# A group norm's sums taken through memory instead of the matrix engine, PSUM emptied ahead of other work, and some products issued in halves

## The chip, the cores and the metric

The kernel runs on one core of a Trainium2 chip. The metric is the device time of one execution in microseconds (us). Engines are named as in the profile: PE (TensorE, matmuls), PEld (its weight loads), DVE (VectorE), ACT (ScalarE), POOL (GpSimd) and SP (SyncE, which issues most DMAs). All data is float32. A float32 matmul appears in the profile as two passes (two MATMUL records) and two weight loads.

## The reference

Sixteen elements of 256 channels by 1024 positions go through two layers. Cut to what matters:

```python
# layer 0: attention of 4 heads of 64 over 1024 positions, biases, residual
q, k, v = split(xs @ w_proj + b_proj)
x = softmax(q k^T * 64**-0.5) v @ w_out + b_out + xs
# layer 1
x = x + attention(group_norm(x, gn1_w, gn1_b), 8 heads of 32, proj, phys_bias)
h = gelu(mlp_w1 @ group_norm(x, gn2_w, gn2_b) + mlp_b1)     # 1024 hidden channels
x = x + mlp_w2 @ h + mlp_b2
# group_norm: 32 groups of 8 channels, mean and variance over 8 x 1024 values,
#             (x - mu) / sqrt(var + 1e-5) * w + b
```

The norm that the change touches is the first group_norm, between the two attentions.

## The kernel before

**Tiling.** Channels lie on partitions: 256 channels are two chunks (cc or ch) of 128 partitions, positions two halves (t) of TB = 512. The loop over the elements b holds, for each, attention a (layer 0), a stretch of full-array products, and attention b (layer 1); the MLP of element b - 1 is computed inside the turn of element b. Elements 1 to 14 are treated alike (`seven`); the first and the last have their own paths. In the attentions PE works in small tiles of the array (64x64, 32x64, 128x32); in the stretch between them it works with the whole array (128*128).

**The stretch between the attentions.** On PE it holds, for an inner element: the first half of the MLP of the element before (`begin`, `middle`, `finish`, four units i each, `products_of`, L1209), the output projection of attention a (`out_proj`, L381), the two small products of the norm, and then the query and key projections of the next element's layer 0 ("a") and of this element's layer 1 ("b").

**Projections by seven products.** `qk_by_seven` computes the 2x2 blocks of queries and keys with seven block products instead of eight. A piece is named layer, product, chunk: a20 is product 2 of chunk 0 for layer a. Each piece is one matmul of 128x512 (`mm`, L1108) and what follows: products 1 and 7 start a PSUM area, 6, 2, 4, 5, 3 accumulate into one. ACT copies two of the results aside (L1137, L1141) and one within PSUM (L1132); keys leave by ACT (L1116, L1118), queries by DVE (L1122 for b, L1124 for a). The inputs' sums t1 to t4 are made by DVE (`input_sums`, L1088 to L1091). The order of the pieces is written out in the main loop as a string of names.

**The norm.** `out_proj` adds the residual (L821) and takes statistics per channel (L825). `group_norm` joins them (`bn_aggr`, L894), and a product with a matrix of group averages, `gavg`, gives each channel the mean of its group: `gm_g` for the means, then on DVE the deviation, squared and added (L906 to L908), then `gv_g` for the variances (L915). `pow` on POOL (L916) gives the reciprocal root, three small DVE instructions scale and shift (L918 to L922), and four DVE instructions of 128x512 write the normed element (L928).

**The MLP's hidden units.** `finish(i)` adds two PSUM results on DVE (L1265, L1266), applies gelu to them on ACT (L1224), and forms two differences on DVE (L1285).

**What sets the order.** `Later` holds callbacks for a number of steps (`wait` in `group_norm`), so instructions are emitted between the pieces. A scheduler of the framework then orders each engine's instructions by its own estimates; `keep_in_program_order` and `issue_after` bind it. Each engine executes its own list in that order, and waits for the others by semaphores. SP's DMAs are one such list: between the last transfers of attention a (`row_a`, `d_a`, L422 and L427) and the load of the MLP's second weights (L315) it issues nothing.

**PSUM.** Three double areas (`wide`) and two single banks (`bank`) are handed round; a matmul that takes an area waits until the instructions that read it have run.

Of the kernel before, what the change touches and what calls it, by code (L numbers as in the profile page):

```python
# [8 lines left out]
F32 = mybir.dt.float32  # L9
I32 = mybir.dt.int32  # L10
AF = mybir.ActivationFunctionType
ALU = mybir.AluOpType
AX = mybir.AxisListType

P = 128
# [268 lines left out]
def first_pass(ctx, tc, x, out, k):  # L284
# [3 lines left out]
    HC = k["m1b"].shape[1]  # L288
    later = Later()
# [579 lines left out]
    def group_norm(key, src, stats, gw, gb, tag, out_tile, wait, then=None):  # L869
# [21 lines left out]
        def means():  # L891
            mv = small.tile([P, CC, 2], F32, tag="mv", name=f"mv_{key}")
            for cc in range(CC):
                nc.vector.bn_aggr(mv[:, cc, :], stats[:, cc].rearrange("p t k -> p (t k)"))  # L894
            mean_c = small.tile([P, CC], F32, tag="mean_c", name=f"mean_c_{key}")
# [15 lines left out]

        def apply():
            rstd = small.tile([P, CC], F32, tag="rstd", name=f"rstd_{key}")
            for sl, ps in averages(f"gv_{key}", st["tv"], False):
                nc.vector.tensor_scalar(rstd[sl], ps, EPS, None, ALU.add)  # L915
            nc.gpsimd.tensor_tensor(rstd, rstd, k["mhalf"], ALU.pow)  # L916
# [3 lines left out]
            nc.vector.tensor_mul(ma, st["mean"], a)  # L920
# [3 lines left out]
            out_tile.append(y)  # L924

# [10 lines left out]
            for t in range(NT):  # L936
                for cc in range(CC):
                    part(cc, t)
# [7 lines left out]
    def qkv(key, D, src, weights, b_qk, qT, kT, v_dst):  # L946
        def qk(ch, which, t):
            ps = single(f"qk_{key}_{ch}_{which}_{t}")
            for cc in range(CC):
                product(  # L950
                    ps,
                    weights(cc, which)[:, ch * P : (ch + 1) * P],
                    src[:, cc, t * TB : (t + 1) * TB],
                    start=(cc == 0),
                    stop=(cc == CC - 1),
                )
# [34 lines left out]
    def qkv_0(b, xb):  # L991
# [5 lines left out]
        def v():  # L997
# [7 lines left out]
            k["bqk"], q, kk, v,  # L1005
        )

    def qkv_1(b, xn):
# [6 lines left out]
            None, q, kk, lambda: v,  # L1015
# [67 lines left out]
    def input_sums(key, y):  # L1083
# [7 lines left out]
        nc.vector.tensor_sub(t4, b21, t2)  # L1091
        return dict(t1=t1, t2=t2, t3=t3, t4=t4, b11=b11, b21=b21, b22=b22)

    made_k = []

    def qk_by_seven(key, block, s, x, q, kk, bias=None):
# [10 lines left out]
        def mm(to, w, right, first):  # L1107
            ins = nc.tensor.matmul(  # L1108
                to, w, x[right], start=first, stop=True, skip_group_check=not first
            )  # L1110
            if ps:
                tc.keep_in_program_order(ins)
# [7 lines left out]
        def leave_q(to, what, more, ch):  # L1120
            if bias is None:
                nc.vector.tensor_add(to, more, what)  # L1122
            else:
                nc.vector.scalar_tensor_tensor(  # L1124
                    to, what, bias[:, 0, ch : ch + 1], more, ALU.add, ALU.add
                )
# [12 lines left out]
        def p6(ch):  # L1139
            mm(ps[ch][1], s[:, ch, 1], "t2", False)  # L1140
            nc.scalar.copy(aside_for()[:, 2 * ch + 1], ps[ch][1])  # L1141
# [5 lines left out]
        def p4(ch):  # L1147
            mm(ys[ch], block(0, ch, 1), "t4", False)
# [732 lines left out]
```

## Time and profile before

| | |
|---|---|
| median of 3 runs | 3586.73 us (3586.65 to 3588.13) |
| the profiled execution's own time | 3587.91 us |
| its span | 3586.1 us |
| PE busy | 3573.3 us, 35713 passes |
| DVE busy | 2785.1 us |
| ACT busy | 2288.7 us |
| POOL busy | 220.1 us |
| granted PE clock | 1.0 |
| DMA | 198.07 MB, mean 55 GB/s |

The page has the busy time of each engine, the span in 40 slices, the DMA queues, the chain of work that ended last, and groups of instructions with the idle time ahead of them and what ended it. In a timeline, each line has the start (us from the span's start), the duration, the engine, the source line, and the tiles written and read; in brackets the idle time ahead and its releaser. An end of a matmul is modelled; the starts are used here.

### The profile page before, as it was taken

What the parts mean: (1) busy time and instruction counts of PE and PEld (TensorE: products, weight loads), DVE (VectorE), ACT (ScalarE), POOL (GpSimd) and SP (SyncE); (2) the same over time, 40 slices, a digit from 0 to 9 for tenths busy, and PEclk for the clock granted to TensorE, in tenths of its full rate; (3) what the DMA queues carried; (4) which work ended last, traced back from release to release, by engine and by line L of the source; (5) the groups of instructions that cost most, each with busy time, mean ns of one, the idle gap of its engine ahead of it and who ended that gap; (6) DMA issues with size and microseconds to landing.
All of it is one profiled execution on the core that took longest, in us unless ns stands there. A gap on an engine that the chain in (4) does not pass through costs nothing.

```text
span 3586.1 us, 82054 instructions
## 1 busy us (share of the span) xinstructions
PE 3573.3 (100%) x35713; PEld 1479.0 (41%) x35713; DVE 2785.1 (78%) x3188; ACT 2288.7 (64%) x3186; POOL 220.1 (6%) x319
## 2 busy tenths in 40 slices
PE   9999999999999999999999999999999999999999
PEld 4334344343444434444344443444434444344434
DVE  5786877868788687886868878688786877869787
ACT  5665757567575675856658566585765757657573
POOL 4000000001000010000000000000000100000000
PEclk9999999999999999999999999999999999999999
DMA  4011312213122131221312213121121211213100
GB/s 134 8 58 33 82 51 40 72 39 82 45 44 68 39 82 45 52 65 35 82 45 52 66 34 81 45 55 63 39 77 45 55 63 43 72 45 64 52 28 28
DMA packets 81606, 198.07 MB, mean 55 GB/s; under 512 B 38006, under 2 KB 38774, under 8 KB 75094
## 3 DMA queue, kind: packets, MB, share of 16 engines
q1 hardware_dynamic: 71860, 164.13, 15.0%
q0 software_dynamic: 7632, 28.21, 5.1%
q8 instruction: 282, 4.62, 0.5%
q14 instruction: 86, 0.70, 0.1%
q10 hardware_dynamic: 1746, 0.40, 0.1%
HBM read 125.59 MB, written 22.27 MB: 41 GB/s over the span
## 4 chain that ended last, share of the span: by engine, by line
PE 93%; DVE 4%; DMA 1%; issue 1%; SPq 0%; ACT 0%; DVEq 0%
PE s_b L642 13%; PE s_a L458 13%; PE acc_a L481 12%; PE acc_b L696 12%; PE m L1209 9%; PE m L381 9%; PE qk_a L1108 3%; PE qk_b L1108 3%; PE v_b L381 3%; PE j L381 3%; PE v_a L381 3%; PE o L381 3%; PE qk7y_b L1108 1%; PE qk7y_a L1108 1%; DVE es_b L670 1%
## 5 line engine op out<-in xcount | busy, mean ns | idle before, releaser
L655 ACT ACTIVATE e_b<-s_b 128x1024 f32<-128x1024 f32 (+1 forms) x1280 | 982.1, 864 | 135.3 <-PE s_b L642 135.3
L670 DVE TENSOR_TENSOR es_b<-es_b,e_b 128x2048 f32<-128x2048 f32 (+1 forms) x460 | 881.5, 1934 | 105.0 <-ACT e_b L655 88.6
L468 ACT ACTIVATE e_a<-s_a 128x1024 f32<-128x1024 f32 x512 | 521.2, 1025 | 359.1 <-PE s_a L458 356.3
L458 PE MATMUL s_a<-q,k 64*64 64x512 f32 x4096 | 544.3, 593 | 0.0
L481 PE MATMUL acc_a<-e_a,v 64*64 64x512 f32 x4096 | 540.1, 589 | 0.0
L642 PE MATMUL s_b<-q,k 32*64 32x512 f32 x8192 | 523.4, 600 | 2.7 <-ACT v L978 1.3
L495 DVE TENSOR_TENSOR es_a<-es_a,e_a 128x1024 f32<-128x1024 f32 x384 | 471.8, 1229 | 63.7 <-ACT e_a L468 42.9
L696 PE MATMUL acc_b<-e_b,v 128*32 128x512 f32 x4096 | 492.1, 598 | 0.0
L381 PE MATMUL m<-g,w 128*32 128x256 f32 (+1 forms) x6432 | 401.8, 384 | 0.0
L381 PEld LDWEIGHTS m<-g,w 128*32 128x32 f32 x6432 | 218.7, 111 | 205.0 <-issue 54.8
L481 PEld LDWEIGHTS acc_a<-e_a,v 64*64 64x64 f32 x4096 | 187.9, 133 | 251.5 <-issue 222.9
L642 PEld LDWEIGHTS s_b<-q,k 32*64 32x64 f32 x8192 | 175.8, 130 | 247.5 <-issue 122.4
L458 PEld LDWEIGHTS s_a<-q,k 64*64 64x64 f32 x4096 | 175.8, 133 | 247.0 <-issue 216.5
L696 PEld LDWEIGHTS acc_b<-e_b,v 128*32 128x32 f32 x4096 | 108.5, 109 | 351.5 <-ACT e_b L655 194.7
L1209 PE MATMUL m<-gn_h,w 128*128 128x512 f32 x504 | 238.3, 601 | 0.7 <-DVE g L1237 0.7
L670 DVE TENSOR_TENSOR es_b<-e_b,e_b 128x2048 f32<-128x2048 f32 (+1 forms) x72 | 147.0, 2051 | 105.8 <-ACT e_b L655 105.8
L1285 DVE TENSOR_TENSOR g<-g,g 128x512 f32<-128x512 f32 (+1 forms) x184 | 193.5, 1062 | 2.1 <-PE m L381 0.8
L1209 PE MATMUL m<-hs,w 128*128 128x512 f32 x380 | 176.0, 592 | 0.0
L1224 ACT ACTIVATE g<-g,m1b 128x512 f32<-128x512 f32 x128 | 91.6, 721 | 94.1 <-DVE g L1265 67.2
L1209 PEld LDWEIGHTS m<-gn_h,w 128*128 128x128 f32 x504 | 91.8, 190 | 113.9 <-issue 99.1
L1122 DVE TENSOR_TENSOR q<-qk7p_b,qk_b 128x512 f32<-128x512 f32 x28 | 19.3, 688 | 134.5 <-PE qk_b L1108 134.5
L1224 ACT ACTIVATE g<-m,m1b 128x512 f32<-128x512 f32 x128 | 81.0, 684 | 66.8 <-PE m L1209 66.8
(251 smaller groups left out, 3667.6 us busy)
## 6 DMA issues: line engine op xcount, KB each, us to landing
w<-w_kept SPq DMA_DIRECT2D x30, 1792.0 KB
packed_b<-es_b SPq DMA_DIRECT2D x42, 512.0 KB
packed_b<-es_b POOLq DMA_DIRECT2D x42, 512.0 KB, 6.3
rd_b<-row_b SPq DMA_DIRECT2D x252, 64.0 KB
out_dram<-x SPq DMA_DIRECT2D x63, 256.0 KB
d_a<-row_a SPq DMA_DIRECT2D x62, 256.0 KB
x<-in_x_dram SPq DMA_DIRECT2D x30, 512.0 KB
qk<-qk_kept SPq DMA_DIRECT2D x14, 1024.0 KB
```

What stands on the lines that cost most here:

```text
L381: nc.tensor.matmul(o[sl], w[:, sl], r, **flags)
L458: nc.tensor.matmul(s[h : h + HALF, g, :], kT[g * D : (g + 1) * D, c, kb * P + h : kb * P + h + HALF], qT[g * D : (g + 1) * D, c, t * TB : ...
L468: nc.scalar.activation(e, s, AF.Exp, scale=float(D) ** -0.5)
L481: nc.tensor.matmul(accs[i][h][g * D : (g + 1) * D, :], v[h * HALF : (h + 1) * HALF, kb, c * 2 + g], e[h * HALF : (h + 1) * HALF, g, :], st ...
L495: spread_out["es"] = nc.vector.tensor_add(sums[i], held[i] if kb == 1 else sums[i], e)
L642: nc.tensor.matmul(outs[g][h : h + HALF, :], kT[g * D : (g + 1) * D, c, k0 : k0 + HALF], qT[g * D : (g + 1) * D, c, t * TB : (t + 1) * TB] ...
L655: spread_out["exp"] = nc.scalar.activation(to, s, AF.Exp, scale=float(D) ** -0.5)
L670: ins = nc.vector.tensor_add(d, (d if kb else es[0][:, g : g + step]), es[m][:, g : g + step])
L696: nc.tensor.matmul(acc[g * D : (g + 1) * D, :], v[:, kb + m, c * G + g], es[m][:, g, :], start=(m == 0), stop=(m == 1),)
L1108: ins = nc.tensor.matmul(to, w, x[right], start=first, stop=True, skip_group_check=not first)
L1209: nc.tensor.matmul(ps, blocks[1][number - 1][:, i * P : (i + 1) * P], inputs[b][number], start=first, stop=True, skip_group_check=not first,)
L1285: (nc.vector.tensor_add if plus else nc.vector.tensor_sub)(d, d, more)
```

## The change

- `group_norm` gets a branch for the inner elements: the statistics of the 128 channels (16 bytes each) are written to memory, and read back so that each channel has those of its group's eight channels. DVE then forms means and variances itself; `gm_g` and `gv_g` are not computed on PE there. The four instructions that write the normed element are issued later, next to `input_sums`.
- For units 2 and 3 of the MLP's hidden half the four gelus and the four differences are put off: the gelus until after the second copy of product 6 of layer a, the differences until after the last query of layer a has left PSUM. The sum t4 of layer b follows them (layer a's is also put off, to where it was).
- Products 6, 4 and 5 of both layers, and 3 of layer b, are issued as two matmuls of 256 columns: 14 per element. The query and key projections of the first element (16 products of layer a, 8 of layer b) are so too.

```diff
...
     B, C, S = x.shape
     CC, SB, NT = C // P, S // P, S // TB
     HC = k["m1b"].shape[1]
+    GSZ = C // GROUPS
     later = Later()

     act = ctx.enter_context(tc.tile_pool(name="act", bufs=1))
...
         return issue


-    def group_norm(key, src, stats, gw, gb, tag, out_tile, wait, then=None):
+    def group_norm(
+        key, src, stats, gw, gb, tag, out_tile, wait, then=None, over_memory=False
+    ):
         st = {}


...
             mv = small.tile([P, CC, 2], F32, tag="mv", name=f"mv_{key}")
             for cc in range(CC):
                 nc.vector.bn_aggr(mv[:, cc, :], stats[:, cc].rearrange("p t k -> p (t k)"))
+            if over_memory:
+                return around(mv)
             mean_c = small.tile([P, CC], F32, tag="mean_c", name=f"mean_c_{key}")
             nc.vector.tensor_copy(mean_c, mv[:, :, 0])
             st.update(mv=mv, mean_c=mean_c)
...
             st.update(mean=mean, tv=dv)
             later.after(1 if cols[0] == P else 5, apply)

+        def around(mv):
+            row = dram.tile([P // GSZ, GSZ * CC * 2], F32, tag="stats", name=f"row_{key}", bufs=2)
+            nc.sync.dma_start(row.rearrange("g (j f) -> (g j) f", j=GSZ), mv)
+            n = GSZ * CC
+            full = work.tile([P, TB], F32, tag="full", name=f"of_{key}", bufs=2)
+            nc.sync.dma_start(
+                full[:, : 2 * n], row.unsqueeze(1).to_broadcast([P // GSZ, GSZ, 2 * n])
+            )
+            later.after(wait, lambda: from_group(
+                full[:, : 2 * n].rearrange("p (j c f) -> p f c j", c=CC, f=2),
+                full[:, 2 * n : 3 * n].rearrange("p (c j) -> p c j", c=CC),
+            ))
+
+        def from_group(of_group, dv):
+            means, variances = of_group[:, 0], of_group[:, 1]
+            mean = small.tile([P, CC], F32, tag="mean", name=f"mean_{key}")
+            tc.keep_in_program_order(nc.vector.tensor_reduce(mean, means, AX.X, ALU.add))
+            nc.vector.scalar_tensor_tensor(
+                dv, mean.unsqueeze(2).to_broadcast([P, CC, GSZ]), -1.0 / GSZ, means,
+                ALU.mult, ALU.add,
+            )
+            nc.vector.tensor_mul(dv, dv, dv)
+            nc.vector.tensor_add(dv, dv, variances)
+            rstd = small.tile([P, CC], F32, tag="rstd", name=f"rstd_{key}")
+            nc.vector.tensor_reduce(rstd, dv, AX.X, ALU.add)
+            nc.vector.tensor_scalar(rstd, rstd, 1.0 / GSZ, EPS, ALU.mult, ALU.add)
+            st.update(mean=mean)
+            scale_by(rstd, 1.0 / GSZ)
+
         def apply():
             rstd = small.tile([P, CC], F32, tag="rstd", name=f"rstd_{key}")
             for sl, ps in averages(f"gv_{key}", st["tv"], False):
                 nc.vector.tensor_scalar(rstd[sl], ps, EPS, None, ALU.add)
+            scale_by(rstd, None)
+
+        def scale_by(rstd, share):
             nc.gpsimd.tensor_tensor(rstd, rstd, k["mhalf"], ALU.pow)
             a = rstd
             nc.vector.tensor_mul(a, rstd, gw)
             ma = small.tile([P, CC], F32, tag="gma", name=f"gma_{key}")
-            nc.vector.tensor_mul(ma, st["mean"], a)
+            if share is None:
+                nc.vector.tensor_mul(ma, st["mean"], a)
+            else:
+                nc.vector.scalar_tensor_tensor(ma, st["mean"], share, a, ALU.mult, ALU.mult)
             c = ma
             nc.vector.tensor_sub(c, gb, ma)
             y = act.tile([P, CC, S], F32, tag=tag, name=f"gn_{key}")
             out_tile.append(y)
+
+            def all_parts():
+                for t in range(NT):
+                    for cc in range(CC):
+                        part(cc, t)

             def part(cc, t):
                 sl = slice(t * TB, (t + 1) * TB)
...
             if nc.in_order:
                 then(y, part)
                 return
-            for t in range(NT):
-                for cc in range(CC):
-                    part(cc, t)
+            if over_memory:
+                mlp_made["norm"] = all_parts
+                return
+            all_parts()
             if then:
                 then(y)

...

-    def qkv(key, D, src, weights, b_qk, qT, kT, v_dst):
+    def qkv(key, D, src, weights, b_qk, qT, kT, v_dst, halves):
         def qk(ch, which, t):
             ps = single(f"qk_{key}_{ch}_{which}_{t}")
-            for cc in range(CC):
-                product(
-                    ps,
-                    weights(cc, which)[:, ch * P : (ch + 1) * P],
-                    src[:, cc, t * TB : (t + 1) * TB],
-                    start=(cc == 0),
-                    stop=(cc == CC - 1),
-                )
+            size = TB // (2 if halves and cols[0] == P else 1)
+            for c0 in range(0, TB, size):
+                for cc in range(CC):
+                    product(
+                        ps[:, c0 : c0 + size],
+                        weights(cc, which)[:, ch * P : (ch + 1) * P],
+                        src[:, cc, t * TB + c0 : t * TB + c0 + size],
+                        start=(cc == 0),
+                        stop=(cc == CC - 1),
+                    )
             d = (kT if which else qT)[:, ch, t * TB : (t + 1) * TB]
             if b_qk is None:
                 nc.scalar.copy(d, ps)
...
         return (q, kk, v), qkv(
             f"a{b}", D0, xb,
             lambda cc, which: k["wp"][:, cc, which].rearrange("p h d -> p (h d)"),
-            k["bqk"], q, kk, v,
+            k["bqk"], q, kk, v, not b,
         )

     def qkv_1(b, xn):
...
         return (q, kk, v), qkv(
             f"b{b}", D1, xn,
             lambda cc, which: k["wq"][:, cc, which * C : (which + 1) * C],
-            None, q, kk, lambda: v,
+            None, q, kk, lambda: v, not b,
         )

     def attention_0(b, qkv_tiles, xb, norm):
...
         nc.vector.tensor_sub(t3, b22, b12)
         nc.vector.tensor_sub(t1, b12, b11)
         nc.vector.tensor_sub(t2, b22, t1)
-        nc.vector.tensor_sub(t4, b21, t2)
+        sums_4[key] = lambda: nc.vector.tensor_sub(t4, b21, t2)
         return dict(t1=t1, t2=t2, t3=t3, t4=t4, b11=b11, b21=b21, b22=b22)

-    made_k = []
+    made_k, made_q, made_got, sums_4 = [], [], [], {}

     def qk_by_seven(key, block, s, x, q, kk, bias=None):
         ps, ys, got = {}, {}, []
...
         def half(d, ch, t):
             return d[:, ch, t * TB : (t + 1) * TB]

-        def mm(to, w, right, first):
-            ins = nc.tensor.matmul(
-                to, w, x[right], start=first, stop=True, skip_group_check=not first
-            )
-            if ps:
-                tc.keep_in_program_order(ins)
+        def mm(to, w, right, first, parts=1):
+            size = TB // parts
+            for c0 in range(0, TB, size):
+                sl = slice(c0, c0 + size)
+                ins = nc.tensor.matmul(
+                    to[:, sl], w, x[right][:, sl],
+                    start=first, stop=True, skip_group_check=not first,
+                )
+                if ps:
+                    tc.keep_in_program_order(ins)

         def leave_k(to, what, ch):
             if bias is None:
...
             if bias is None:
                 nc.vector.tensor_add(to, more, what)
             else:
-                nc.vector.scalar_tensor_tensor(
+                made_q.append(nc.vector.scalar_tensor_tensor(
                     to, what, bias[:, 0, ch : ch + 1], more, ALU.add, ALU.add
-                )
+                ))

         def p1(ch):
             both = wide(f"qk7_{key}_{ch}", order[1] if ch == 0 and bias is not None else None)
...
             nc.scalar.copy(aside_for()[:, 2 * ch], ys[ch])

         def p6(ch):
-            mm(ps[ch][1], s[:, ch, 1], "t2", False)
-            nc.scalar.copy(aside_for()[:, 2 * ch + 1], ps[ch][1])
+            mm(ps[ch][1], s[:, ch, 1], "t2", False, 2)
+            made_got.append(nc.scalar.copy(aside_for()[:, 2 * ch + 1], ps[ch][1]))

         def p2(ch):
             mm(ps[ch][0], block(1, ch, 1), "b21", False)
             leave_k(half(kk, ch, 0), ps[ch][0], ch)

         def p4(ch):
-            mm(ys[ch], block(0, ch, 1), "t4", False)
+            mm(ys[ch], block(0, ch, 1), "t4", False, 2)
             leave_q(half(q, ch, 0), ys[ch], got[0][:, 2 * ch + 1], ch)

         def p5(ch):
-            mm(ps[ch][1], s[:, ch, 0], "t1", False)
+            mm(ps[ch][1], s[:, ch, 0], "t1", False, 2)
             leave_q(half(q, ch, 1), ps[ch][1], got[0][:, 2 * ch], ch)

         def p3(ch):
-            mm(ps[ch][1], s[:, ch, 3], "b22", False)
+            mm(ps[ch][1], s[:, ch, 3], "b22", False, 2 if bias is None else 1)
             leave_k(half(kk, ch, 1), ps[ch][1], ch)

         return {
...
             rest = gs[1, 1, i]
             nc.vector.tensor_add(unit(0, 0, i), rest, ps[:, 0, :])
             made["added"] = nc.vector.tensor_add(rest, rest, ps[:, 1, :])
-            gelu(0, 0, i, gs[0, 0, i])
-            gelu(1, 1, i, rest)
-            combine((1, 0), (0, 0), False, i)
-            combine((0, 1), (1, 1), False, i)
+            steps = (
+                lambda: gelu(0, 0, i, gs[0, 0, i]),
+                lambda: gelu(1, 1, i, rest),
+                lambda: combine((1, 0), (0, 0), False, i),
+                lambda: combine((0, 1), (1, 1), False, i),
+            )
+            if 2 * i >= n4 and b + 2 < B:
+                for what, fn in zip(("gelus", "gelus", "sums", "sums"), steps):
+                    made.setdefault(what, []).append(fn)
+                return
+            for fn in steps:
+                fn()

         def back_to_exp():
             one = small.tile([P, 1], F32, tag="part", name=f"one_{b}")
...
         later.after(14, load_next)
         xn = []
         seven = 0 < b < B - 1
-        xn_made = []
         run(
             attention_0(
                 b, tiles0, xs[b],
-                lambda st, b=b, xn=xn, seven=seven, xn_made=xn_made: group_norm(
-                    f"g{b}", xs[b], st, k["g1w"], k["g1b"], "res", xn, 2 if b else 1,
-                    xn_made.append if seven else None,
+                lambda st, b=b, xn=xn, seven=seven: group_norm(
+                    f"g{b}", xs[b], st, k["g1w"], k["g1b"], "res", xn,
+                    4 if seven else 2 if b else 1, None, seven,
                 ),
             )
         )
...
             run_pieces(hidden[1:2])
             with tc.issue_after(mlp_made["begun"].ins):
                 sums_0 = input_sums(f"a{b}", xs[b + 1])
+                sums_4[f"a{b}"]()
             made = {"a": qk_by_seven(
                 f"a{b}", qk_block_0, qk_parts[:, 0], sums_0, *tiles0[:2], k["bqk"]
             )}
...

         if seven:
             with tc.issue_after(mlp_made["added"].ins):
-                sums_1 = input_sums(f"b{b}", xn_made[0])
+                mlp_made.pop("norm")()
+                sums_1 = input_sums(f"b{b}", xn[0])
             made["b"] = qk_by_seven(
                 f"b{b}", qk_block_1, qk_parts[:, 1], sums_1, *tiles1[:2]
             )
...
             def pieces(names):
                 return [made[n[0]][int(n[1]), int(n[2])] for n in names.split()]

-            run_pieces(pieces(
-                "a10 a70 a11 a60 a40 a61 a50 a41 a51 a20 b10 a21 a30 b60 a31 b11 b70"
-                " b50 b61 b71 b20"
-            ))
+            run_pieces(pieces("a10 a70 a11 a60 a40 a61 a50 a41 a51"))
+            with tc.issue_after(made_got[-1].ins):
+                for fn in mlp_made.pop("gelus"):
+                    fn()
+            with tc.issue_after(made_q[-1].ins):
+                for fn in mlp_made.pop("sums"):
+                    fn()
+                sums_4[f"b{b}"]()
+            run_pieces(pieces("a20 b10 a21 a30 b60 a31 b11 b70 b50 b61 b71 b20"))
             with tc.issue_after(made_k[-1].ins):
                 mlp_made["exp"]()
             run_pieces(pieces("b51 b40 b30 b21 b41") + v[:1] + pieces("b31"))
```

## The prediction

> **What bounds the kernel now.** I read the page first, then the timeline of one inner element's turn from attention a to attention b, then the queue and the DMA packets. The page says that TensorE is never idle at full clock:
>
> ```profile
> PE 3573.3 (100%) x35713; PEld 1479.0 (41%) x35713; DVE 2785.1 (78%) x3188; ACT 2288.7 (64%) x3186; POOL 220.1 (6%) x319
> PEclk9999999999999999999999999999999999999999
> PE 93%; DVE 4%; DMA 1%; issue 1%; SPq 0%; ACT 0%; DVEq 0%
> ```
>
> So time can only come from passes that PE need not make and from holes between passes. An inner element (1 to 14) recurs every 221.61 us where nothing is late; elements with a late transfer take 222.1 to 222.9, longer by the hole itself. PE time is therefore worth its full value. The timeline of element 2, TensorE alone, shows what is there to win:
>
> ```profile
> 515.73 0.28 PE L381 MATMUL gm_g<-mean_c_g,gavg 128*128 128x2 f32 x2
> 515.87 1.10 PE L1209 MATMUL m<-gn_h,w 128*128 128x512 f32 x2
> 516.81 1.02 PE L1209 MATMUL m<-hs,w 128*128 128x512 f32 x2
> 517.67 0.28 PE L381 MATMUL gv_g<-dv_g,gavg 128*128 128x2 f32 x2
> 517.81 1.96 PE L1209 MATMUL m<-gn_h,w 128*128 128x512 f32 x4
> 519.61 3.60 PE L1209 MATMUL m<-hs,w 128*128 128x512 f32 x8
> ...
> 529.91 1.02 PE L1108 MATMUL qk_a<-qk7t_a,qk 128*128 128x512 f32 x2
> 530.93 1.12 PE L1108 MATMUL qk_a<-x,wp 128*128 128x512 f32 x2
> 531.89 1.02 PE L1108 MATMUL qk_b<-gn_g,wq 128*128 128x512 f32 x2
> ```
>
> A full pass starts 0.429 us after the one before, a product (two passes) 0.859. Three places break this. Each group average holds PE for 0.140 (515.73 to 515.87), and the pair behind it takes 0.94 instead of 0.86. And the product at 530.93 comes 1.02 after its predecessor, its own successor 0.96 later. The full timeline names the cause:
>
> ```profile
> 528.15 0.74 DVE L1124 SCALAR_TENSOR_TENSOR q<-qk7y_a,bqk,qk7p_a 128x512 f32<-128x512 f32 x1
> 530.13 0.75 DVE L1124 SCALAR_TENSOR_TENSOR q<-qk_a,bqk,qk7p_a 128x512 f32<-128x512 f32 x1
> 530.93 0.30 PEld L1108 LDWEIGHTS qk_a<-x,wp 128*128 128x128 f32 x2 [0.83 <-DVE q L1124]
> ```
>
> The weight load for a20 (product 2, chunk 0 of layer a) waits until VectorE has emptied its PSUM pair at 530.88.
>
> **The change, part by part** (element 2; 14 elements have it).
> *Averages off TensorE.* Per average 0.029 + 0.111 for its passes and 0.084 on the next pass: 0.224; two of them 0.448; 14 elements: **-6.27 us**.
>
> *The round trip through memory.* The row's nearest relatives on the same queue:
>
> ```profile
> 493.24 0.58 SPq L405 DMA_DIRECT2D sp_a<-d_a  x1
> 498.49 0.32 SPq L422 DMA_DIRECT2D row_a<-inv_a  x1
> 499.89 1.10 SPq L427 DMA_DIRECT2D d_a<-row_a  x2
> ```
>
> row_a<-inv_a is a 128-partition write of 64 B each to memory; the dependent read issues 1.40 us later. sp_a, 128 small pieces, reaches its reader on GpSimd at 495.22, 1.98 after its issue. The statistics are ready at 513.73 (L894 at 513.53, 0.20 long), so the group values arrive near 513.77 + 1.40 + 1.98 = 517.2. [...] VectorE reaches the first norm instruction only after its second L1242: before, that starts at 517.87; without gm_g 0.22 earlier, so it ends at 518.34. I take the rows; the 16 B pieces of the new write are untried here, bounds 3.2 us (the rows at their shortest, 1.39 + 1.83) to 6.6 (a 3.5 us row write, met below, and a slow read of 3.1).
>
> VectorE then has six tiny dependent steps (nearest: 0.16 to 0.25 each, some 0.2 apart: 1.3), pow on GpSimd and three steps as before (518.63 to 519.99: 1.36): done near 521.0. Behind them stand L1265 and L1266 for the last two units, which wait for PE until about 522.8 and end at 524.2; then the four scalings (1.92) to 526.1 and three input sums to 528.1. The four L1285 and t4, which before stood among these, now come after the q results. So q of a40 is emptied 528.1 to 528.8, and a50's, which a20 waits for, by 529.6. On PE, 0.448 earlier, a20's weights are due at 529.9 and must start by about 530.1. **The stall goes**: 0.163 of hole and 0.104 of refilled pipeline, times 14: **-3.74 us**. Late next is a21, which needs a51 emptied: 531.2 against 531.6. The chain's slack: the values may land at 519.15, a round trip of 5.4 us, before a20 slips.
> ACT: the four last gelus now follow two PSUM copies and run about 528.5 to 531.4, in time for k of a20, whose product ends at 531.2. SP: nothing is behind the two new transfers but the weights at 523.24, which wait for PE anyway. GpSimd's order is unchanged.
>
> *Halves.* A 256-column pass takes 0.2157 where the trace has them (v_b), 0.0020 more than half of 0.4294. Two more passes per product: 14 x 14 x 2 x 0.002 = 0.78, and 24 first products 0.10: **+0.88 us**. No wait gets shorter by them: weights for the next product are still due 0.19 before its start.
>
> *What the halves also move: code fetches.*
>
> ```profile
> q8 instruction: 282, 4.62, 0.5%
> 275.60 3.20 DMA row_a<-inv_a
> 279.45 4.02 DMA d_a<-row_a
> ```
>
> [...] Laid over the trace this fits PE: one f32 product on the full array is four PE instructions, and a packet appears whenever PE has passed another 256, some 150 to 190 beyond the multiple. All six row_a writes that took 3.0 to 3.5 us (at 275.6, 469.4, 1607.3, 1801.4, 2939.8, 3133.6) have such a packet within 1.3 us of their issue; the other 26, at 1.4, have none. An element is 4565 PE instructions in the built order, 213 over a multiple, so a fetch meets row_a in elements 1, 7 and 13, where the output projection (0.59, 0.97, 0.44) and the next hidden product (0.34 each) wait, with six refills of 0.10: 3.63 us. The change adds 14 and removes 2 products: 4613 = 18 x 256 + 5. The fetch stays at one place, drifting by 5: in the new order 158 to 226 instructions ahead of the first qk7y_a, which is around 488 to 491 on element 2's scale, clear of sp_a and row_a, and 30 to 98 behind it, clear of the round trip (over by 517.2, a fetch not before 520). **-3.63 us.** Against it: in attention b a fetch beside the rd_b reads delays j in elements 2, 8, 12, 13 (0.36, 0.45, 0.34, 0.04, refills 0.4: 1.6 us). With a fixed place this meets none or many: 0 to 14 x 0.55 = 7.7. In elements whose fetch stood near the new place I see both outcomes; I take 2.1, **+0.5**.
>
> Sum: -6.27 - 3.74 + 0.88 - 3.63 + 0.5 = -12.3. The profiled span, 3586.1, becomes 3573.8; that execution's own time was 3587.91 and the runs' median 3586.73, 0.6 above the span. Forecast **3574.5 us**, own range 3571 to 3578.
>
> **Rivals.** *The round trip is late.* VectorE is strictly in order, and the norm chain now stands ahead of L1265 and of all q results. From 5.4 us on, each microsecond is one of PE in 14 elements; at 6.3 the gain (12.3 / 14 = 0.88) is gone, and at 7.3 the time is 3574.5 + 14 x 1.9 = 3601. For it: row writes of 3.5 us exist and 16 B pieces are smaller than any seen. Against: no other transfer runs on the queue there, and it must be late in nearly every element.
> *The fixed fetch lands badly.* It sits beside the rd_b reads in all elements: +7.7 instead of 2.1, 3580.1. For it: phases are now alike in all 14; against: elements 3 and 9, near the new place, show no wait.
> *The stall only moves.* If emptying is still late, a20 keeps 0.27 and the time is 3578.2.
> *PE's freed time turns into waiting elsewhere*, in attention b, where exponentials feed it: 3586. The element lengths speak against it.
>
> **How the numbers follow.** No more than 0.2% (7.2 us) can be told from no change. Main case 0.66, stall only moves 0.10, bad fetch 0.10, freed time lost 0.04, late round trip 0.10. Faster: main, moved stall and four tenths of the bad fetch, 0.80; same: the rest of it, the lost time and the mildest late trips, 0.11; slower 0.09. The range takes the main case, the moved stall and the bad fetch: 3571 to 3581; outside lie the late trip, the lost time and some tail.
>
> **What would show it.** Right: no gm_g and gv_g in inner elements; 1.72 for the two products around a20; the values' reader on VectorE starting at its predecessor's end, not at a landing; elements of about 220.9 us, all alike, with 1, 7 and 13 no longer. Wrong: a wait of VectorE for the new read, the last units' L1265 later than 523, or j waiting for rd_b in most elements.

## The result: 3575.5 us, 0.32% less, and the profile after

The changed kernel takes 3575.48 us (median of 8 runs, 3574.66 to 3577.18); the kernel before took 3586.84 beside it. The ratio is 0.9968, 95% interval 0.9958 to 0.9978. The profiled execution's span went from 3586.1 to 3574.6.

The page after, its busy times, granted clock, instruction packets and shares of the chain that ended last:

```profile
PE 3562.1 (100%) x36097; PEld 1558.1 (44%) x36097; DVE 2793.2 (78%) x3188; ACT 2286.1 (64%) x3186; POOL 223.4 (6%) x319
PEclk9999999999999999999999999999999999999999
q8 instruction: 285, 4.67, 0.5%
PE 93%; DVE 3%; issue 2%; DMA 1%; SPq 1%; ACT 0%; DVEq 0%
```

TensorE is still never idle at full clock. It has 384 more matmul records and 11 us less busy time. Those are 192 products, 768 TensorE instructions, and the instruction packets rose by three, from 282 to 285. In the mean 254 recorded TensorE instructions lie between two packets, before and after. The timeline of TensorE in element 2, at the places that the prediction showed of before:

```profile
514.39 1.02 PE L1261 MATMUL m<-hs,w 128*128 128x512 f32 x2
515.25 1.88 PE L1261 MATMUL m<-gn_h,w 128*128 128x512 f32 x4
516.96 3.60 PE L1261 MATMUL m<-hs,w 128*128 128x512 f32 x8
...
527.29 1.03 PE L1159 MATMUL qk_a<-qk7t_a,qk 128*128 128x256 f32 x4
528.15 1.02 PE L1159 MATMUL qk_a<-x,wp 128*128 128x512 f32 x2
529.01 1.02 PE L1159 MATMUL qk_b<-gn_g,wq 128*128 128x512 f32 x2
529.87 1.02 PE L1159 MATMUL qk_a<-x,wp 128*128 128x512 f32 x2
```

The averages gm_g and gv_g are gone, and a20 (528.15) and b10 (529.01) start 0.86 us after their predecessors: no hole, and no refill, as the prediction calls the 0.10 us by which the product behind a hole starts later (0.96 instead of 0.86). The queue of SyncE and the timeline of VectorE in the same element show why nothing waits for the new round trip:

```profile
511.56 0.33 SPq L919 DMA_DIRECT2D row_g<-mv_g  x1
512.97 0.55 SPq L922 DMA_DIRECT2D of_g<-row_g  x1
```

```profile
515.45 0.69 DVE L1294 TENSOR_TENSOR g<-g,m 128x512 f32<-128x512 f32 x1 [1.52 <-PE m L1261]
516.05 0.17 DVE L933 TENSOR_REDUCE mean_g<-of_g 128x2 f32<-128x16 f32 x1
...
518.88 0.69 DVE L1317 TENSOR_TENSOR g<-g,m 128x512 f32<-128x512 f32 x1 [0.24 <-PE m L1261]
...
521.92 1.91 DVE L973 TENSOR_SCALAR gn_g<-x,rstd_g,gma_g 128x512 f32<-128x512 f32 x4
...
526.63 0.75 DVE L1176 SCALAR_TENSOR_TENSOR q<-qk_a,bqk,qk7p_a 128x512 f32<-128x512 f32 x1 [0.33 <-PE qk_a L1159]
...
528.35 0.75 DVE L1176 SCALAR_TENSOR_TENSOR q<-qk_a,bqk,qk7p_a 128x512 f32<-128x512 f32 x1
```

The values land at 515.81, 4.25 us after the write was issued; VectorE comes to them at 516.05 without a wait, and the q result that frees a20's PSUM pair has left it at 527.38. What VectorE still waits for in this stretch is TensorE (0.18 to 1.52 us by the brackets) and, within the norm's chain, GpSimd's power (0.81 ahead of 518.09, as before ahead of 519.44).

Element lengths (from the first product of attention a's block to that of the next element) are the finest measure here. Undisturbed ones were 221.61 us and are 220.98; in this execution four are longer by 0.5 to 1.2 us, all four because j, attention b's output projection, waits. Over the whole span, between the two profiled executions:

| | predicted, us | in the traces, us |
|---|---|---|
| undisturbed element, 14 times | -9.23 | 14 x -0.635 = -8.9 |
| of that: averages | -6.27 | -0.45 per element, -6.3 (below) |
| slow row_a writes in elements 1, 7, 13 | -3.63 | -4.1, read from element lengths |
| waits of j, with refills | +0.5 | +1.0 (1.9 before, 2.9 after) |
| behind TensorE's last matmul | none | +0.95 |
| the rest, ahead of element 1 and behind element 14 | +0.1 | -0.4 |
| sum | -12.3 | -11.4 (spans: -11.5) |

The fifth row was in no step of the prediction: from TensorE's last matmul to the end of the span it is 4.92 us before and 5.87 after. The last section says what the other traces show of it.

### The profile page after: what moved, and what is told of

It reads as the page before. It is cut to its first block, busy times and chain, and to the rows that moved or that the text cites. A ratio compares the mean times of both kernels' runs of the same rounds, so it can differ in the third digit from the quotient of the medians.

```text
span 3574.6 us, 82906 instructions
## 1 busy us (share of the span) xinstructions
PE 3562.1 (100%) x36097; PEld 1558.1 (44%) x36097; DVE 2793.2 (78%) x3188; ACT 2286.1 (64%) x3186; POOL 223.4 (6%) x319
## 4 chain that ended last, share of the span: by engine, by line
PE 93%; DVE 3%; issue 2%; DMA 1%; SPq 1%; ACT 0%; DVEq 0%
PE s_a L459 13%; PE acc_a L482 12%; PE s_b L643 12%; PE acc_b L697 11%; PE m L1261 11%; PE m L382 9%; PE qk_b L1159 3%; PE qk_a L1159 3%; PE v_b L382 3%; PE o L382 3%; PE j L382 3%; PE v_a L382 3%; DVE es_b L671 1%; PE qk7y_a L1159 1%; PE qk7y_b L1159 1%
## 5 line engine op out<-in xcount | busy, mean ns | idle before, releaser
L382 PE MATMUL v_a<-wp,x 128*32 128x256 f32 (+1 forms) x1952 | 121.7, 379 | 0.0
L382 PE MATMUL v_b<-wq,gn_g 128*32 128x256 f32 (+1 forms) x1664 | 119.7, 380 | 0.0
```

The lines of the kernel that those rows point to most:

```text
L382: nc.tensor.matmul(o[sl], w[:, sl], r, **flags)
```

## Experiments

Each times one kernel against the kernel before on the same chip. "Clean" is the length of an undisturbed inner element in its trace. The kernel before took 3586.84 beside the change, 3587.16 beside e1 to e4, 3587.86 beside e5 to e8 and 3587.81 beside e9 to e12, so medians of different groups compare to about 1 us only; clean elements, most of which repeat within 0.01 us in a trace, compare more closely.

| run | median, us | ratio to before, 95% | clean element, us |
|---|---|---|---|
| before | 3586.84 | | 221.61 |
| the change | 3575.48 | 0.9958 to 0.9978 | 220.98 |
| e1 no halves | 3577.73 | 0.9963 to 0.9985 | 220.90 |
| e2 halves only | 3585.59 | 0.9985 to 1.0004 | 221.66 |
| e3 not put off | 3598.07 | 1.0018 to 1.0041 | 222.59 |
| e4 norm on TensorE | 3582.65 | 0.9977 to 0.9996 | 221.43 |
| e5 16 first halves | 3574.04 | 0.9946 to 0.9973 | 220.98 |
| e6 other phase | 3578.13 | 0.9960 to 0.9982 | 220.98 |
| e7 one more hop | 3582.48 | 0.9976 to 0.9994 | 221.51 |
| e8 round trip twice | 3594.45 | 1.0009 to 1.0028 | 222.36 |
| e9 all in old places | 3589.32 | 0.9995 to 1.0013 | 221.94 |
| e10 scalings in place | 3581.58 | 0.9973 to 0.9992 | 221.41 |
| e11 the change again | 3574.93 | 0.9951 to 0.9978 | 220.97 |
| e12 16 first halves again | 3574.05 | 0.9948 to 0.9975 | 220.97 |

**e4: the norm back on TensorE.**

```diff
-                    4 if seven else 2 if b else 1, None, seven,
+                    2 if b else 1,
...
-                mlp_made.pop("norm")()
```

> The changed kernel with the norm between the attentions through two averages on TensorE, as before; order and halves stay. By the theory +6.27 for 28 averages, +1.2 to 2.4 because 4621 instructions per element bring a fetch onto row_a in elements 14 and perhaps 13, -1.5 to -2.4 because none stands beside the rd_b reads: 3581.4, range 3580 to 3583. If the averages were hidden in some other wait: 3575.5.

3582.65, inside the range. The clean element is 0.45 us longer than the changed kernel's, against 0.448 worked out from four durations; fourteen make 6.3. The timeline shows the two averages again (gm_g at 514.17, the next pair at 514.31). The waits of j, which I expected gone, were still 2.2 us.

**e3: gelus, sums and t4 not put off.**

```diff
-            if 2 * i >= n4 and b + 2 < B:
+            if False:
...
-        sums_4[key] = lambda: nc.vector.tensor_sub(t4, b21, t2)
+        nc.vector.tensor_sub(t4, b21, t2)
...
-            with tc.issue_after(made_got[-1].ins):
-                for fn in mlp_made.pop("gelus"):
-                    fn()
```

(and the same for the sums and the other calls of t4)

> The changed kernel with the last two units' gelus and sums and both t4 in their old places, that is PSUM not emptied first; norm over memory and halves stay. By the theory the stall of a20 comes back (0.27 us or somewhat more, in 14 elements: +3.7, range +2 to +6): 3579.2. If the norm chain alone had brought the stall away: 3575.5.

3598.07: 22.6 above the changed kernel, where I expected 3.7, and slower than the kernel before. The stall is where I said, but a20 starts 1.52 us late (1.35 of it idle by the bracket), where the kernel before had 0.16. VectorE and TensorE in element 2 of this kernel:

```profile
520.89 0.69 DVE L1317 TENSOR_TENSOR g<-g,m 128x512 f32<-128x512 f32 x1 [0.23 <-PE m L1261]
...
524.77 0.69 DVE L1345 TENSOR_TENSOR g<-g,g 128x512 f32<-128x512 f32 x1
525.38 0.54 DVE L973 TENSOR_SCALAR gn_g<-x,rstd_g,gma_g 128x512 f32<-128x512 f32 x1
525.83 0.69 DVE L1345 TENSOR_TENSOR g<-g,g 128x512 f32<-128x512 f32 x1
526.43 1.45 DVE L973 TENSOR_SCALAR gn_g<-x,rstd_g,gma_g 128x512 f32<-128x512 f32 x3
...
530.87 0.74 DVE L1176 SCALAR_TENSOR_TENSOR q<-qk_a,bqk,qk7p_a 128x512 f32<-128x512 f32 x1
```

```profile
531.67 1.12 PE L1159 MATMUL qk_a<-x,wp 128*128 128x512 f32 x2 [1.35 <-DVE q L1176]
```

From 520.89 on VectorE has hardly any idle time. Before the change, the four scalings ran while the last units' products were still being made:

```profile
520.03 1.92 DVE L928 TENSOR_SCALAR gn_g<-x,rstd_g,gma_g 128x512 f32<-128x512 f32 x4
521.86 0.68 DVE L1265 TENSOR_TENSOR g<-g,m 128x512 f32<-128x512 f32 x1
```

In e3 they stand behind those sums, because the change also moved the scalings (the norm's last step is called together with the input sums). Two runs take that apart. (Gelus, sums and t4 were put off together in every run; what each of the three is worth alone was not tried.)

**e9 and e10: the scalings in their old place**, in e9 together with e3's edit, in e10 alone.

```diff
-            if over_memory:
-                mlp_made["norm"] = all_parts
-                return
             all_parts()
...
-                mlp_made.pop("norm")()
```

> The changed kernel with everything on VectorE and ScalarE in its old place: last gelus, sums and t4 not put off (as in the run before that did this), and the four scalings of the norm right behind its chain, no longer behind the last units' sums. VectorE's order is then that of the kernel before, with the norm over memory. The run without the putting off alone had a20 wait 1.35 us. By the theory that the change itself moves 1.9 us of scalings into VectorE's busy stretch, and that the putting off pays for that and for the old stall, the scalings run again where VectorE waits for TensorE; the norm chain ends 0.7 us later than before and TensorE comes 0.45 earlier, but a20's q result stands one sum further ahead: a20 waits 0.3 to 0.8 us, in all 3575.5 + 7, range 3578.5 to 3586.5. If the scalings' place does not matter: 3598.

> The changed kernel with the four scalings alone back behind the norm chain; gelus, sums and t4 stay put off. By the theory VectorE has the same work ahead of the q results and waits for TensorE anyway: no change, 3575.5, range 3574 to 3577. If the place of the scalings costs or brings something by itself: 3 us or more either way.

e9: 3589.32, 8.8 below e3 (0.65 in the clean element, 9.1 in 14). So the scalings' place accounts for about half of the 18.9 that e3 lies above its expectation, and e9 is 2.8 above its own range. e10: 3581.58, 6.7 above the kernel of e11 beside it, where I expected no change. Both have a wait that I had not expected. Weight loads, VectorE and TensorE of e10 in element 2:

```profile
522.81 0.30 PEld L1156 LDWEIGHTS qk_a<-x,wp 128*128 128x128 f32 x2 [1.00 <-DVE g L1315]
```

```profile
519.05 1.92 DVE L973 TENSOR_SCALAR gn_g<-x,rstd_g,gma_g 128x512 f32<-128x512 f32 x4
520.89 1.27 DVE L1314 TENSOR_TENSOR g<-g,m 128x512 f32<-128x512 f32 x2
522.08 1.27 DVE L1315 TENSOR_TENSOR g<-g,m 128x512 f32<-128x512 f32 x2
```

```profile
521.62 1.02 PE L1156 MATMUL qk7y_a<-qk7t_a,qk 128*128 128x512 f32 x2
522.81 1.12 PE L1156 MATMUL qk_a<-x,wp 128*128 128x512 f32 x2 [0.17 <-DVE g L1315]
523.77 1.03 PE L1156 MATMUL qk_a<-qk7t_a,qk 128*128 128x256 f32 x4
```

With the scalings first, VectorE finishes with one of the hidden layer's PSUM pairs only at 522.77 (the end of the first of the two L1315), and a11, the third block product of this list, takes that pair. a11 starts 1.19 us after its predecessor and the next product 0.96 after a11: 0.43 per element, all of the difference in clean elements (221.41 to 220.98). That wait isn't in the kernel before, whose norm chain ends earlier. In e9 it is there too (0.33 and a refill of 0.10), followed by smaller ones up to a21, 0.96 in all. a20, which I had expected to stall in e9, waits 0.03.

The six orders side by side, clean element in us:

| | all in old places | gelus, sums, t4 put off | these and the scalings | scalings alone |
|---|---|---|---|---|
| averages on TensorE | 221.66 (e2) | 221.43 (e4) | | |
| norm over memory | 221.94 (e9) | 221.41 (e10) | 220.98 | 222.59 (e3) |

(all with halves). The norm over memory alone makes an element 0.28 us longer, 3.9 in 14. Putting off alone saves 0.23, both without moving the scalings 0.25. Only all three together save 0.68.

**e7 and e8: a longer round trip.** e7 copies the statistics once in SBUF first; e8 goes through memory twice.

```diff
+            nc.sync.dma_start(mv_2, mv)
-            nc.sync.dma_start(row.rearrange("g (j f) -> (g j) f", j=GSZ), mv)
+            nc.sync.dma_start(row.rearrange("g (j f) -> (g j) f", j=GSZ), mv_2)
```

(e7; in e8 the row is written from mv, read back into mv_2, and mv_2 written to a second row)

> The changed kernel with one more transfer ahead of the round trip: the statistics are first copied to another place in SBUF by the same queue, and the row is written from there. Values land 1.9 to 2.1 us later, some 7.3 from the statistics. In the changed kernel's trace VectorE has 0.3 us before the values are late, and behind that 0.55 of waits for TensorE and 0.56 to 0.6 until a20's weights are due, 1.45 in all. By the theory a20 waits 0.45 to 0.65 us in 14 elements, and each refill of 0.1: 3575.5 + 9, range 3580 to 3588. If the round trip is off the path by a wider margin: 3575.5.

> The changed kernel with the round trip made twice: row written, read back as the statistics, written to a second row, and this one read as group values. Values land 3.4 to 4.1 us later. By the theory everything past 1.45 us of slack is TensorE's, 14 times (1.95 to 2.65 and a refill of 0.1): 3575.5 + 33, range 3602 to 3614. If the round trip is off the path: 3575.5.

e7: 3582.48, inside the range. Queue, VectorE and TensorE in element 2:

```profile
511.77 0.50 SPq L922 DMA_DIRECT2D of_g<-mv_g  x1
513.46 0.33 SPq L923 DMA_DIRECT2D row_g<-of_g  x1
514.86 0.55 SPq L924 DMA_DIRECT2D of_g<-row_g  x1
```

```profile
517.60 0.18 DVE L935 TENSOR_REDUCE mean_g<-of_g 128x2 f32<-128x16 f32 x1 [1.26 <-DMA of_g<-row_g]
```

```profile
528.78 1.12 PE L1161 MATMUL qk_a<-x,wp 128*128 128x512 f32 x2 [0.26 <-DVE q L1178]
```

Now VectorE waits for the values (1.26) and a20 for VectorE (0.26). The values land 5.6 us behind the element's first product instead of 3.9 (medians), and an element is 0.53 longer, 0.10 of it a refill. So a late round trip would have cost what the rival says. Of the 1.65 us that the values come later, some 1.2 were free.

e8: 3594.45, below its range. The values land at 8.0, but an element is only 1.38 longer, with 1.12 of wait at a20. I had taken VectorE's order as fixed. The framework's scheduler lays it when the kernel is built, and with a longer trip it set the last units' sums ahead of the norm chain: in e8 the chain's first instruction runs at 522.79, behind three of the four sums, and waits for no transfer. What a late value costs with the order held fixed was not tried.

**e1 and e2: the halves.** e1 takes them out of the change, e2 adds them alone to the kernel before.

```diff
         def mm(to, w, right, first, parts=1):
-            size = TB // parts
+            size = TB
...
-            size = TB // (2 if halves and cols[0] == P else 1)
+            size = TB
```

> The changed kernel with every product in one piece again (512 columns), the rest as it is. By the theory of code fetches: an element is 4557 TensorE instructions, so the fetch moves by 51 from element to element and meets the row_a write in elements 1, 6 and perhaps 11 (2 to 3 times 1.21 us = +2.4 to +3.6), stands beside the rd_b reads only in elements 3 and 12 (waits of j 0 to 1.0 instead of 2.4), and the shorter list of passes gives 0.88 back: 3575.5 + 3.0 - 1.9 - 0.9, about 3575.7, range 3574.5 to 3577. If halves do nothing but cost their passes: 3574.6 and no slow row_a write. If the halves themselves bring a good part of the gain: over 3578.

> The kernel before with the halves alone: 14 products per element and 24 first ones; norm on TensorE and the order of before. An element is 4621 TensorE instructions, 13 over a multiple of 256. By the theory: row_a meets a fetch in element 14 and perhaps 13 instead of in 1, 7, 13 (-3.6 + 1.2 to 2.4), j waits almost nowhere (-1.6 to -1.0), 0.88 for the passes: 3586.8 - 2.5, 3584.3, range 3583 to 3586. If fetches have no part in it: 3587.7.

e1: 3577.73, 0.7 above the range; its interval overlaps the change's. What separates the theories is in the trace. The chain of waits and TensorE's timeline in element 6:

```profile
1381.47 3.47 DMA row_a<-inv_a
...
1385.53 3.97 DMA d_a<-row_a
```

```profile
1390.87 3.70 PE L382 MATMUL o<-res_a,wo 128*128 128x512 f32 x8 [0.58 <-DVE res_a L575]
...
1399.03 1.98 PE L1261 MATMUL m<-gn_h,w 128*128 128x512 f32 x4 [0.17 <-DVE g L1289]
```

The output projection and the next hidden product wait, as they did before in elements 1, 7 and 13. In e1 they wait in elements 1, 6 and 11, and nowhere else: the three that the count of TensorE instructions had named. In the changed kernel no element has it. In element 1, where the prediction's lines have 3.20 us for the write, its dependent read is now issued after 1.52:

```profile
275.30 0.32 SPq L423 DMA_DIRECT2D row_a<-inv_a  x1
276.82 1.11 SPq L428 DMA_DIRECT2D d_a<-row_a  x2
```

The fourteen traces together sharpen when a fetch matters. Outside the first element they have 420 writes of row_a. Twenty took 2.7 to 3.7 us until the dependent read was issued, and each of these has a packet of the instruction queue that began 0.7 to 1.6 us after the write's issue. Of the other 400 one has such a packet (e4, 1.47 us). Fourteen have one that began 0.5 to 1.5 us before their issue, and they took only 1.4 to 1.8.

The clean element of e1 is 0.075 shorter than with halves, so halves cost 1.05 in 14 elements, against 0.78.

e2: 3585.59, inside the range, though not told apart from no change. Its trace has one wait of the output projection instead of three, in element 13, and 2.1 us of waits of j that I had expected gone.

**e5, e6 and e12: the place of the code fetches alone.** e5 and e12 are one kernel, whose later TensorE instructions stand 32 places earlier; e6 moves the fetches by 120. In e6 the first element's hidden products are issued in two halves, and that element's hidden layer no longer has the reference's values. They run inside the turn of element 1; the turns of elements 2 to 14 have the same work.

```diff
-            size = TB // (2 if halves and cols[0] == P else 1)
+            two = halves and cols[0] == P and len(halved) < 16
+            size = TB // (2 if two else 1)
+            if two:
+                halved.extend(range(CC))
```

(e5 and e12)

```diff
-        for _ in range(n):
+        for _ in range(8):
             nc.tensor.matmul(
-                ps[:, : what.shape[1]], what[:, :P], what, start=True, stop=True
+                ps[:, :192], what[:, :P], what[:, :192], start=True, stop=True
...
+                size = TB // (1 if b else 2)
```

(e6)

> The changed kernel with 16 of the 24 first products in halves instead of 24. Nothing else differs after the first 20 us, but every later TensorE instruction stands 32 places earlier, so each code fetch comes 32 instructions later in its element: near 115 to 116 and 123 to 124 us behind the first product of attention a's block instead of 114.3 and 121.9. By the theory of code fetches the rd_b reads are clear of it in all 14 elements, row_a and the round trip too: waits of j gone, 3575.5 - 2.4 = 3573.1, range 3572 to 3575. If the waits of j come from something else: 3575.5.

> The changed kernel with the same work in elements 1 to 14, but 28 hidden products of the first element in halves and the 3 warm-up products in 8 smaller ones, so that from element 2 on every code fetch comes 120 instructions later than in the changed kernel, some 15 to 16 us ahead of the first block product in elements 2 to 9, where row_a is written; in elements 10 to 14 at -20. By the theory of code fetches the row_a write takes 3.0 to 3.5 us in up to 8 elements and each costs about 1.0 us of TensorE; waits of j go: 3575.5 + 8 - 2.4 + 0.1 = 3581.2, range 3578 to 3585. If the phase of the fetches does not matter: 3575.6.

> The changed kernel itself, beside the next one on the same chip: 3575.5, range 3574.5 to 3577.

> 16 of the 24 first products in halves, again, beside the changed kernel. By the theory of code fetches about 2 us below it, range 1 to 3, with elements of 220.98 us alike and at most two waits of j. If the first run of it was chance: no difference.

e6: 3578.13, the low end of its range. The write of row_a took 2.9 to 3.5 us in elements 5, 6 and 7, and 1.4 to 1.9 in all later and earlier inner ones: three of the eight. So the phase does decide, and moving it brings back slow writes that the change had taken away; but the count of instructions had named all eight.

e5 and e12: 3574.04 and 3574.05, 1.4 below the change's first median and 0.9 below e11; e5 is inside its range, e12 just short of its 1 to 3. Neither is clearly told apart from the change. All 13 element lengths in e12 are 220.97 or 220.98, with one wait of j (0.50) in element 14. But the second trace of the unchanged change, e11, has only 0.28 of such waits, with a fetch at 121 to 123 us in every element, as in the first, which had 2.04. And in e5 the fetches of elements 8 to 13 stayed at 121.5 to 122 although they are 32 instructions later. What makes j wait is therefore not settled: a fetch beside the rd_b reads is there in executions with and without the wait. In the first trace of the change, timeline of TensorE and VectorE in element 2:

```profile
637.12 1.92 PE L382 MATMUL j<-res_b,wpj 128*32 128x512 f32 x16 [1.01 <-DVE res_b L780]
```

```profile
636.37 0.69 DVE L780 TENSOR_TENSOR res_b<-res_b,rd_b 128x512 f32<-128x512 f32 x1 [3.46 <-DMA rd_b<-row_b]
```

The last of four reads landed 4.2 us after its issue; in e11 it is issued at the same place in the element and lands 1.8 us earlier. The waits differ between executions of one program; that they make the spread of the change's runs (3574.7 to 3577.2) is likely, but wasn't measured.

## Why the prediction was right, point by point

- *The time*, 3574.5, is 1.0 below the median measured and inside its own range; the sum of the parts was 0.8 too large. That it came so close is partly luck. In the first trace of the change the elements and row_a add up to -13.0 against -12.9 predicted, and that is the working; but the end of the span (+0.95), the rest (-0.4 for +0.1) and the waits of j (+1.0 for +0.5) happen to cancel in part, and in the second trace j stands at -1.2.
- *Averages off TensorE* (-6.27): right. e4 gives 0.45 per element for 0.448.
- *"The stall goes"* (-3.74): right for the change as a whole, wrong as a part that could be had alone. "Late next is a21" holds in the changed kernel: a51's result has left its pair at 529.10 (the line at 528.35 above), and a21's first weights load at 529.44, 0.34 later; a20 has 0.56. But the prediction placed the scalings behind the last units' sums and saw a20 come free without seeing that this place is needed. Beside the longer norm chain, the scalings' old place makes a11 wait (e10, 6.0 in 14 elements), and moving them without putting off the sums makes a20 wait (e3). In e4 against e2, where the norm is on TensorE, putting off saves 0.23 per element, 3.2 against 3.74: the halves had already shortened that wait to 0.24 with its refill, although the prediction said that they would shorten none.
- *Round trip* (values near 517.2, limit 5.4): on the element's scale it ended 0.5 to 1.2 later than predicted, because the dependent read takes 2.66 us (median; 1.98 assumed from sp_a). The write took the 1.40 assumed in nine elements and 1.9 to 2.6 in five; in these five the read took only 2.0 to 2.2, so the two together stay within 4.0 to 4.6. Hidden in all 14 nevertheless. The limit is borne out by e7: 5.8 us from the first issue, 0.4 past the limit, cost 0.43 and a refill.
- *Halves* (+0.88, of it 0.78 in the elements): 1.05 there, so a quarter was missing.
- *Code fetches* (-3.63): right in kind, with two slips in the lines read. The sixth packet began 1.4 us from its write's issue, not within 1.3, and two of the 26 quick writes do have a packet near (at 246.5 and 2910.7), begun 1.2 and 0.6 us before their issue; what the six long writes share is a packet that begins 0.8 to 1.4 us after it. The 256 instructions to a packet hold in the mean, by 254 recorded ones between two packets of the kernel before (25 to 405 in single cases) and 768 more for three more packets; "150 to 190 beyond the multiple" holds for 174 of the 282 packets only. The recurrence that the counts gave is in the traces: long writes every six elements at 4565 instructions (1, 7, 13), every five at 4557 (e1: 1, 6, 11). No row_a write in the changed kernel's inner elements takes over 1.9 us, and e1 brings the long writes back in the elements named. The size was 4.1, because the element after the hole lost a little more than hole and refill.
- *Waits of j* (+0.5): +1.0 in the first trace of the change, -1.2 in the second. A term with such a spread belonged in the range, not in the sum; that it belongs to fetches is not shown.
- *Rivals*: the round trip is not late; it would be from about 1.2 us beyond what the change uses (e7). A stall that only moves appears when a part of the change is left out (e9, e10). TensorE's freed time was not lost elsewhere: the clean element is shorter by 0.63.

## To carry to other kernels

Price the parts of a change together when they share a queue of instructions: here taking work off the bound engine alone made an element 0.28 us longer (e9 against e2), because the same engine that does the new work also empties the PSUM pairs that the bound engine waits for. For each instruction moved on such an engine, list the PSUM buffers emptied behind it and the first product that takes each one, in order; the one with the least time to spare sets the slack, and it need not be the one that stalls now. Small waits that recur every few loop turns (here every six, in e1 every five) are worth laying against the count of instructions before they are put down to chance.

## What was not expected of the hardware

- A read of 16 rows of 128 B from memory, each to eight partitions, took 2.66 us from issue to landing (1.96 to 2.92), a copy of 128 pieces within SBUF (e7) 1.67; a write of 128 pieces of 16 B to memory took 1.38 at its shortest, as long as one of 64 B pieces (row_a).
- The span ends 5.87 us after TensorE's last matmul instead of 4.92. The norm over memory isn't the reason: e6, e7 and e8 have it and end after 4.82 to 4.91. The eight traces with a long end (5.87 to 6.22) have 4421 records on VectorE's list, the six with a short one (4.82 to 4.99) 4425 or 4435. In the long ones VectorE's branch at L271 starts 1.03 us after that matmul instead of 0.67, and three packets of 8 KB on the instruction queue q14 begin 1.9 to 2.6 us after it, instead of one or two. That the end depends on where VectorE's code falls fits all 14 traces, but no run tested it. It makes e6, e7 and e8 about 1 us shorter beside the change, which has nothing to do with what they test.
- Packets of the instruction queue come at the same place in attention b of 13 elements (114.3 us) although the program's count moves by 5 per element or by 32 at once (e5). What holds them there was not tried.
